# The last unit four heads at once, the last batch left by groups and transposes, the gate's choice moved, and buffers of their own for loaded weights

## Chip, cores, metric

The kernel runs on one core of one Trainium2 chip. The metric is the device time of one execution in microseconds; lower is better. All data are float32.

## What is computed

The input x is 8 batches of 1024 tokens of width 256. Cut to what matters:

```
x = x + 0.5 * ffn(layernorm(x))        # 8 experts, top-2 gate, capacity CAP
x = x + attn(layernorm(x))             # causal, 16 heads of 16
x = x + 0.5 * ffn(layernorm(x))

ffn:  probs = softmax(x @ gate_w.T); the two best experts of each token
      keep  = counts <= CAP            # CAP = 1.25 * 8192 / 8 = 1280
      an expert with counts > CAP gives nothing at all
attn: q,k,v = x@Wq.T+bq, x@Wkv.T+bkv;  softmax(q k^T / 4, causal) v;  @Wo.T + bo
```

Two choices per token make 16384 choices over 8 experts, 2048 on the mean, so with such data every expert is over its capacity and both ffn terms are zero. The kernel decides this on the chip: it counts the choices of both gates, and only where some expert is kept does it run the expert path, under `tc.If`. The profiled execution runs the attention and both counts, and no expert path.

## The kernel before

`attention` walks 32 **units**, four per batch b; unit u is group g = u mod 4, of four heads. A unit has 24 **steps**. `m_steps(u+1)` finds each query row's greatest score for the next unit: TensorE score tiles `sm`, then VectorE maxima (`first`, or a fused mask-add and maximum whose result lands in `top`). `settle` transposes the maxima (`pm`) and subtracts them from the queries (`qE`). `e_steps(u)` makes the scores again, transposed (`sc`), ScalarE takes the exponential into `pT`, GpSimd zeroes the part above the diagonal, and TensorE sums values and the softmax denominator into `pav`, for two halves `hf` of 512 query columns each.

A head is 16 wide plus one row for the maximum, so it takes 32 of TensorE's 128 rows. In a step, `scores(h)` is called for h = 0, 1 (two heads, pair `pr`), and between them `ms[k](h)` (two heads of the other pair). Both together use all four groups of 32 rows. In the last unit (u = 31) there is no next unit, so `ms[k]` is `None` and two heads alone are in a step. The values of a pair of steps are `owed` and done two and three steps later.

Other work goes **beside** the steps: generators that yield a number (wait so many steps), `PIECE` (a piece of TensorE work, begun when a step allows one) or `REST`. `Beside.step` runs what is due; `Beside.finish` runs a work to its end at once. The generators are `prepare`, `enter`, `values_of`, `residual` (load, normalise, project to values), `project` (queries and keys of two groups, spread to heads by DMAs from a tile `packed`), `gate_first` (first gate's choice), `leave` (divide by the softmax sums, project by Wo, add to x, store) and `regate` (second gate's choice). `choose` is the choice itself: maximum, softmax, then twice a best value, its lowest index and a one-hot row; some 20 VectorE instructions on 128x64 or 128x32 elements, parted by nine yields.

`leave(b, hf)` reads the 16 heads back from DRAM (`att_d`): sums, reciprocal, to DRAM (`inv_d`), back broadcast (`inv`), GpSimd multiply (`on`), then four `px` products over two chunks of 8 heads each. It is added at step 9 of g = 3 for the first half, and at step 2 of the next batch for the second. For the last batch, b = 7, the second half's `leave` and `regate` run after all units, by `drain`, followed by `any_kept` twice and the flag.

The opening sets up constants, `weights` loads and transposes Wk, Wq, Wv, Wo, and batch 0 is normalised and projected (two halves), before unit -1 with the `m_steps` of unit 0. Inside `attention` all of TensorE's, VectorE's, ScalarE's and GpSimd's instructions are kept in program order (`InOrder`); DMAs go in order on the queue of the engine that issues them. In the opening the query heads of the first group are spread by ScalarE's queue, all other heads by SyncE's:

```python
elif k < 4:
    (nc.sync if dsts is kTs else scalar).dma_start(out=to, in_=head)
else:
    others.append((to, head))
```

The loaded weights `wsb` share tag `packed`, four buffers of 128x512, with `project`. PSUM has six score banks and two of tag `bank` for all else.

Of the kernel before, what the change touches and what calls it, by code (L numbers as in the profile page):

```python
# [10 lines left out]
F32 = mybir.dt.float32  # L11
# [7 lines left out]
P = 128  # L19
# [81 lines left out]
def macaron_kernel(  # L101
# [59 lines left out]
    def mm(name):  # L161
# [16 lines left out]
    row16 = const.tile([P, 4], F32, name="row16")  # L178
    gpsimd.memset(row16, 0.0)
    gpsimd.affine_select(  # L180
        out=row16, in_=row16, pattern=[[-32, 4]], compare_op=ALU.not_equal, fill=1.0, base=-HD, channel_multiplier=1
    )
    one16 = const.tile([P, 1], F32, name="one16")
    vector.tensor_reduce(one16, row16, AX.X, ALU.max)
# [23 lines left out]
    def weights(pool, bank, matmul, transpose):  # L208
        def load(src, queue):
            wsb = pool.tile([P, DC, D], F32, tag="packed", name="wsb", bufs=4)  # L210
            queue.dma_start(out=wsb, in_=src.rearrange("(c p) d -> p c d", p=P))
            return wsb
# [15 lines left out]
        vector.tensor_scalar(bqT, bqT, QSCALE, None, ALU.mult)  # L228
# [98 lines left out]
    def choose(rp, tag, n, lg):  # L327
# [12 lines left out]
        yield 1  # L340
        sm = new("sm", (P, n))
# [7 lines left out]
        vector.scalar_tensor_tensor(key, key, 1e30, lc, ALU.mult, ALU.min)  # L349
        yield 1  # L350
        ohs = []
        for k in range(2):
            best = new("best", (P, n))
            vector.tensor_reduce(best, key, AX.X, ALU.max)
            cand = new("cand")
            vector.tensor_tensor(cand, key, over_e(best), ALU.is_equal)
            yield 1

            vector.scalar_tensor_tensor(
                cand, cand, -100.0, iota_e.unsqueeze(1).to_broadcast([P, n, E]), ALU.mult, ALU.add  # L360
            )
            first = new("first", (P, n))
            vector.tensor_reduce(first, cand, AX.X, ALU.min)
            yield 1
            oh = new(f"oh{k}")
            vector.tensor_tensor(oh, cand, over_e(first), ALU.is_equal)
            if k == 0:
                vector.scalar_tensor_tensor(key, oh, -1e32, key, ALU.mult, ALU.add)
            ohs.append(oh)
            yield 1  # L370
        both = new("both")
        vector.tensor_tensor(both, ohs[0], ohs[1], ALU.add)
        return prob, ohs, both
# [15 lines left out]
    def any_kept(layer, tally, ps):  # L389
# [5 lines left out]
        vector.tensor_scalar(counts, counts, float(CAP), None, ALU.is_le)  # L395
        some = route.tile([P, 1], F32, tag=f"some{layer}", name=f"some{layer}")
        vector.tensor_reduce(some, counts, AX.X, ALU.max)
        return some

    def flag(some, what):  # L400
        word = route.tile([P, 1], I32, tag="word", name=f"word_{what}")
        vector.tensor_copy(word, some)
        return nc.values_load(word[0:1, 0:1], min_val=0, max_val=1)


    def routing(layer, logits, wts, slots, idx):
        with tc.tile_pool(name=f"rt{layer}", bufs=1) as rp:
# [7 lines left out]
            prob, ohs, both = run(choose(rp, f"r{layer}", NT, logits))  # L415
# [247 lines left out]
    def attention(run_no, src, dst, gate0, logits, tally):  # L663
# [3 lines left out]
        with stack:  # L667
# [125 lines left out]
            def gate_first(b):  # L793
                if gate0 is not None:
                    lg = gate0[0][:, b * TB : (b + 1) * TB, :]
                    both = (yield from choose(ap_route, f"f{b}", TB, lg))[2]
                    vector.tensor_tensor(gate0[1], gate0[1], both, ALU.add)
# [3 lines left out]
            def project(u, apart, parts=(0, 512)):  # L801
# [3 lines left out]
                for s0 in parts:  # L805
                    others = []
                    for wT, bT, dsts, scale in ((wkT, bkT, kTs, 1.0), (wqT, bqT, qTs, QSCALE)):
# [14 lines left out]
                        for k in range(8):  # L822
# [3 lines left out]
                            if apart:  # L826
                                nc.sync.dma_start(out=to, in_=head)
                            elif k < 4:
                                (nc.sync if dsts is kTs else scalar).dma_start(out=to, in_=head)
# [51 lines left out]
            def e_steps(u):  # L881
# [28 lines left out]
                def values(hf, jb, pTs, part):  # L910
# [21 lines left out]
                    if jb == 4 * hf + 3 and part == 0:  # L932
# [70 lines left out]

            def regate(b, j0, j1):
# [10 lines left out]
                both = (yield from choose(ap_route, f"g{b}_{j0}", n, lg))[2]  # L1015
                vector.tensor_tensor(tally[:, j0:j1], tally[:, j0:j1], both, ALU.add)
# [60 lines left out]
            owed, light = deque(), deque()  # L1077
# [3 lines left out]
            for u in range(-1, NU):  # L1081
# [20 lines left out]
                if u > 0 and g == 0:  # L1102
                    beside.finish(valuing)
                    beside.add(gate_first(b))
# [10 lines left out]
                for k in range(STEPS) if u >= 0 else ():  # L1115
# [16 lines left out]
                    if g == 3 and u >= 0 and k == 9:  # L1132

                        beside.add(chain(leave(b, 0), regate(b, 0, HT) if b + 1 == B else ()))
# [14 lines left out]
                    beside.step(k in long_steps or u in (0, NU - 1) or beside.pending() > 1)  # L1149
# [5 lines left out]
            drain(leave(B - 1, 1))  # L1155
            drain(regate(B - 1, HT, TB))
            for e in (pe, vector, scalar, gpsimd):
                e.keep = False

# [3 lines left out]
    attention(0, x, out, (logits[0], tallies[0]), logits[1], tallies[1])  # L1163

    def kept_at_all(layer, tally):
        with ExitStack() as stack:
            ffn_banks(stack, f"count{layer}")
            return any_kept(layer, tally, acc(f"cnt{layer}"))

    somes = [kept_at_all(f"{k}", tallies[k]) for k in range(2)]  # L1170
    either = route.tile([P, 1], F32, name="either")
    vector.tensor_tensor(either, somes[0], somes[1], ALU.max)
    with tc.If(flag(either, "either") > 0):

        with tc.If(flag(somes[0], "0") > 0):
            feed_forward(0, logits[0], x, xw_d)
            tally = tally_tile("1b")
            attention(1, xw_d, out, None, logits[1], tally)
            vector.tensor_copy(somes[1], kept_at_all("1b", tally))
# [42 lines left out]
```

## Time and profile before

| | us |
|---|---|
| median of 3 runs | 1482.22 (1478.57 to 1483.34) |
| the profiled execution | 1481.55 |
| its span, first to last instruction | 1479.8 |
| TensorE busy | 1411.9 |
| VectorE busy | 1061.8 |
| ScalarE busy | 789.9 |
| GpSimd busy | 397.1 |

The table is of one execution. "Busy" is the sum of an engine's instructions; TensorE's ends are modelled, so its busy share does not say that it is at its peak. The chain of waits starts at the last instruction and goes back from each to what released it. In the groups and the timeline nearly every line of code reads L37, since a helper issues all instructions; the names of the tiles tell them apart. A number after x counts instructions, for TensorE in the chain weight loads and products together.

### The profile page before, as it was taken

The page shows a single profiled execution, that of the slowest core. Times are in us where ns is not written, and L with a number is a line of the kernel's source. Part 1 is how long each engine was busy: PE and PEld are TensorE (multiplying, and loading weights), DVE is VectorE, ACT ScalarE, POOL GpSimd, SP SyncE. Part 2 cuts the span into 40 slices and gives each one's busy share as a digit, 9 for nine tenths or more (in the row PEclk, how much of TensorE's full clock was granted, in tenths as well). Part 3 has the DMA queues.
Part 4 walks back from the last instruction along what each step waited for, and adds up shares of the span by engine and source line. Part 5 has one row for each costly group of instructions (what it writes and reads, how often), then busy time and mean ns, then how long its engine had stood idle before and what let it go on. Part 6 is the DMA issues. An engine that isn't in the chain of part 4 may idle for free.

```text
span 1479.8 us, 38173 instructions
## 1 busy us (share of the span) xinstructions
PE 1411.9 (95%) x14760; PEld 554.8 (37%) x14760; DVE 1061.8 (72%) x3395; ACT 789.9 (53%) x1790; POOL 397.1 (27%) x713
## 2 busy tenths in 40 slices
PE   5999999999999999999999999999999999999972
PEld 2434333343434333343333334343333434334320
DVE  2857678777877767777787777877677777778622
ACT  2255555555555565555555555555655556555640
POOL 2015114241143313142141411433131421321121
PEclk9999999999999999999999999999999999999995
DMA  4010111211021210212112111212112111121010
GB/s 138 9 37 23 37 33 43 67 58 47 29 62 55 69 37 32 64 41 80 31 46 66 58 45 30 64 49 72 37 32 62 42 51 31 47 66 37 23 61 32
DMA packets 58224, 71.93 MB, mean 49 GB/s; under 512 B 15912, under 2 KB 33456, under 8 KB 58032
## 3 DMA queue, kind: packets, MB, share of 16 engines
q1 hardware_dynamic: 56688, 68.60, 15.6%
q8 instruction: 118, 1.93, 0.5%
q10 hardware_dynamic: 1344, 0.79, 0.2%
q14 instruction: 74, 0.61, 0.1%
HBM read 26.88 MB, written 25.69 MB: 36 GB/s over the span
## 4 chain that ended last, share of the span: by engine, by line
PE 86%; DVE 6%; POOL 2%; ACT 2%; DMA 2%; issue 1%; SPq 0%; ACTq 0%; DVEq 0%; POOLq 0%
PE sc L37 39%; PE pav L37 20%; PE pq L37 8%; PE sm L37 7%; PE pv L37 4%; PE px L37 4%; DVE sm L37 2%; PE pm L37 2%; DVE qE L37 2%; PE pta L37 1%; ACT pT L37 1%; DMA att_d<-att 1%; POOL rstd_a L37 1%; POOL xa L37 1%; POOL pT L37 1%
## 5 line engine op out<-in xcount | busy, mean ns | idle before, releaser
L37 ACT ACTIVATE pT<-sc 128x512 f32<-128x512 f32 (+3 forms) x1536 | 669.3, 488 | 550.0 <-PE sm L37 448.0
L37 PE MATMUL sm<-kT,qT 32*128 32x512 f32 (+3 forms) x3072 | 786.1, 536 | 1.7 <-DVE top L37 0.5
L37 PE MATMUL sc<-qE,kT 32*128 32x512 f32 (+3 forms) x3072 | 736.6, 534 | 1.3 <-ACT pT L37 1.3
L37 POOL TENSOR_SCALAR_AFFINE_SELECT pT<-pT 128x256 f32<-128x256 f32 x512 | 207.1, 407 | 987.7 <-ACT pT L37 984.4
L37 DVE TENSOR_REDUCE first<-sm 128x1 f32<-128x512 f32 x512 | 328.7, 684 | 150.2 <-PE sm L37 147.2
L37 PE MATMUL pav<-pT,vaug 128*32 128x256 f32 (+2 forms) x5120 | 386.7, 371 | 1.7 <-POOL pT L37 1.7
L37 PEld LDWEIGHTS sc<-qE,kT 32*128 32x128 f32 x3072 | 261.4, 183 | 336.8 <-ACT pT L37 237.4
L37 DVE CUSTOM_DVE_ANT_0 sm<-sm,causal,first 128x256 f32<-128x256 f32 (+3 forms) x512 | 262.1, 555 | 94.2 <-PE sm L37 86.0
L37 PEld LDWEIGHTS sm<-kT,qT 32*128 32x128 f32 x3072 | 299.3, 184 | 23.6 <-DVE top L37 11.8
L37 DVE CUSTOM_DVE_ANT_0 sm<-sm,causal 128x256 f32<-128x256 f32 (+3 forms) x512 | 241.3, 514 | 72.0 <-PE sm L37 52.4
L37 PEld LDWEIGHTS pav<-pT,vaug 128*32 128x32 f32 x5120 | 102.7, 108 | 333.1 <-issue 221.6
L37 DVE DVE_READ_ACCUMULATOR2_ANT top<- 128x1 f32 x1024 | 144.5, 141 | 0.0
L37 PE MATMUL px<-woT,on 128*32 128x264 f32 x1024 | 81.8, 402 | 20.1 <-POOL on L37 18.2
L37 PE MATMUL pv<-wvT,xnT 128*32 128x264 f32 x1024 | 82.1, 393 | 1.7 <-DVE qE L37 1.6
L37 PE MATMUL pq<-xnT,wkT 128*32 128x512 f32 x512 | 69.7, 621 | 3.7 <-ACT xnT L37 3.7
L37 POOL TENSOR_SCALAR xn_a<-xa,mv_a,rstd_a 128x256 f32<-128x256 f32 x56 | 67.7, 1222 | 19.1 <-PE pta L37 19.0
L37 PE MATMUL pq<-xnT,wqT 128*32 128x512 f32 x512 | 66.8, 596 | 0.8 <-ACT packed L37 0.8
L37 PEld LDWEIGHTS px<-woT,on 128*32 128x32 f32 x1024 | 30.4, 112 | 55.2 <-POOL on L37 20.3
L37 DVE TENSOR_TENSOR qE<-qT,pm 128x512 f32<-128x512 f32 x64 | 43.5, 679 | 3.2 <-PE pm L37 2.3
L37 POOL TENSOR_TENSOR on<-on,inv 128x512 f32<-128x512 f32 x32 | 40.6, 1270 | 11.2 <-DMA inv<-inv_d 11.2
L37 PEld LDWEIGHTS pv<-wvT,xnT 128*32 128x32 f32 x1024 | 29.8, 110 | 36.6 <-issue 15.5
L37 POOL TENSOR_TENSOR xa<-xa,bo_all 128x528 f32<-128x528 f32 x32 | 41.8, 1307 | 2.8 <-issue 2.3
(113 smaller groups left out, 552.3 us busy)
## 6 DMA issues: line engine op xcount, KB each, us to landing
att_d<-att SPq DMA_DIRECT2D x64, 256.0 KB
kT<-packed SPq DMA_DIRECT2D x256, 32.0 KB
on<-att_d SPq DMA_DIRECT2D x32, 256.0 KB
inv<-inv_d SPq DMA_DIRECT2D x32, 256.0 KB
out_dram<-xa SPq DMA_DIRECT2D x16, 512.0 KB
qT<-packed SPq DMA_DIRECT2D x248, 32.0 KB
xa<-in_L_attn_x_dram SPq DMA_DIRECT2D x7, 1024.0 KB
xa<-in_L_attn_x_dram SPq DMA_DIRECT2D x2, 512.0 KB
```

The lines of the kernel that those rows point to most:

```text
L37: i = call(*args, **kwargs)
```

## The change

1. The last unit runs pairs of steps: the scores of both pairs `pr`, four heads, then the values owed from the pair of steps before.
2. The last batch leaves by groups of heads. `leave_first` divides and projects heads 0 to 7 in unit 30, both halves; `divided` treats heads 8 to 11 by the same way over DRAM; the last group, heads 12 to 15, does not go over DRAM: `leave_last` copies `pav`, transposes it, divides with the sum beside the values, transposes back and projects. The first half of it runs in unit 31, with its `regate` behind it.
3. `choose` finds the first one-hot row from `lc == 0` rather than from `key`, while the exponential runs; it has six yields instead of nine. `both` is gone, each one-hot row is added to the tally by itself. `gate_first(b)` of a later batch is added at step 9 of g = 0 rather than at its start.
4. In the opening: `one16` is made by GpSimd alone, the scaling of `bqT` goes from VectorE to GpSimd, the query heads are spread by SyncE's queue, and `wsb` has four buffers of its own.
5. The counts: `fewest` is taken inside `attention`, for the first gate ahead of the second half's `leave_last`, and the flag is written as an integer at once.

```diff
-    row16 = ...
-    vector.tensor_reduce(one16, row16, AX.X, ALU.max)
+    gpsimd.memset(one16, 0.0)
+    for k in range(4):
+        gpsimd.affine_select(out=one16, in_=one16, pattern=[[0, 1]], ..., base=-32 * k - HD, ...)
...
-            wsb = pool.tile([P, DC, D], F32, tag="packed", name="wsb", bufs=4)
+            wsb = pool.tile([P, DC, D], F32, tag="wsb", name="wsb", bufs=4)
...
-        vector.tensor_scalar(bqT, bqT, QSCALE, None, ALU.mult)
+        gpsimd.tensor_scalar(bqT, bqT, QSCALE, None, ALU.mult)
...
 choose:
+        def lowest(oh):
+            vector.tensor_tensor(cand, cand, iota_e..., ALU.add)
+            first = new("first", (P, n))
+            vector.tensor_reduce(first, cand, AX.X, ALU.min)
+            vector.tensor_tensor(oh, cand, over_e(first), ALU.is_equal)
+        vector.tensor_scalar(cand, lc, 0.0, -100.0, ALU.is_equal, ALU.mult)
+        lowest(ohs[0])
+        yield 1
         sm = new("sm", (P, n))
...
+        vector.scalar_tensor_tensor(key, ohs[0], -1e32, key, ALU.mult, ALU.add)
         yield 1
-        for k in range(2): ...
+        best = ...; cand = (key == best)
+        yield 1
+        vector.tensor_scalar(cand, cand, -100.0, None, ALU.mult)
+        lowest(ohs[1])
+        yield 1
+        return prob, ohs
...
 project:
-                            if apart:
+                            if apart or k < 4:
                                 nc.sync.dma_start(out=to, in_=head)
-                            elif k < 4:
-                                (nc.sync if dsts is kTs else scalar).dma_start(out=to, in_=head)
...
 values:
-                    if jb == 4 * hf + 3 and part == 0:
+                    if u == NU - 1 and jb == 4 * hf + 3:
+                        if part == 0:
+                            last.append(pav.pop(hf))
+                    elif jb == 4 * hf + 3 and part == 0:
...
+            def divided(b, hf, h0, h1, on, waits):
+                att_d, n = att_ds[b, hf], h1 - h0
+                sums = ...
+                yield waits[0]
+                nc.sync.dma_start(out=sums[: 8 * n], in_=att_d[h0:h1, HD, :]...)
+                nc.sync.dma_start(out=on[: HD * n], in_=att_d[h0:h1, :HD, :])
+                yield waits[1]
+                vector.reciprocal(sums[: 8 * n], sums[: 8 * n])
+                nc.sync.dma_start(out=inv_d[:n]..., in_=sums[: 8 * n])
+                yield waits[2]
+                nc.sync.dma_start(out=inv[: HD * n, 0, :], in_=inv_d[:n]...to_broadcast([n, HD, 512]))
+                yield waits[3]
+                gpsimd.tensor_tensor(on[: HD * n], on[: HD * n], inv[: HD * n, 0, :], ALU.mult)
+                yield 2
+
+            def leave_first(b, hf):
+                ...
+                yield from divided(b, hf, 0, 8, on[:, 0], (2, 3, 3, 3))
+                for i in range(HT):
+                    yield PIECE
+                    matmul_cols(px[:, : D + E], on[:, 0, i * P : (i + 1) * P], woT[:, 0, :])
+                    vector.tensor_tensor(xb[:, j, :], px[:, : D + E], xb[:, j, :], ALU.add)
+
+            def leave_last(b, hf, pav, copies):
+                gpsimd.memset(normed[:, :, : P // 2], 0.0)
+                for k in range(2):
+                    copies[k](att[:, k * 256 : k * 256 + 256], pav[:, k * 256 : k * 256 + 256])
+                yield PIECE
+                for i in range(4):
+                    transpose(pt[:, i * P : (i + 1) * P], att[:, i * P : (i + 1) * P])
+                vector.reciprocal(inv, heads[:, :, :, HD])
+                for i in range(4):
+                    vector.tensor_tensor(normed[:, i, P // 2 :]..., heads[:, i, :, :HD], inv..., ALU.mult)
+                yield PIECE
+                for i in range(4):
+                    transpose(pt[:, i * P : (i + 1) * P], normed[:, i])
+                for k in range(2):
+                    copies[k](on[P // 2 :, 1, cols], pt[P // 2 :, cols])
+                for i in range(4):
+                    yield PIECE
+                    matmul_cols(px[:, : D + E], on[:, 1, i * P : (i + 1) * P], woT[:, 1, :])
+                    vector.tensor_tensor(xb[:, j, :], px[:, : D + E], xb[:, j, :], ALU.add)
+                    ln_stats(xb, j, *gate_lns[b])
+                nc.sync.dma_start(out=dst[b, rows]..., in_=xb[:, hf * HT : hf * HT + HT, :D])
...
 the units:
+                for k in range(0, STEPS, 2) if u == NU - 1 else ():
+                    then = es[k + 1][1]
+                    for h in range(2):
+                        es[k][0](h)
+                        es[k + 1][0](h)
+                    owed.append((0, then, 0)); owed.append((0, then, 1))
+                    while len(owed) > 2:
+                        _, then, part = owed.popleft()
+                        then(part)
+                    if k == 0:
+                        beside.add(divided(b, 1, 8, 12, ons[1][:, 1], (1, 3, 3, 3)))
+                    if k == 2:
+                        beside.add(settle(u, 1), first=True)
+                    if k == 8:
+                        beside.finish(dividing)
+                        copies = (vector.tensor_copy, vector.tensor_copy)
+                        beside.add(chain(leave_last(b, 0, last.pop(), copies), regate(b, 0, HT)), first=True)
+                    for begin in (True, False):
+                        ...
+                        beside.step(begin)
-                for k in range(STEPS) if u >= 0 else ():
+                for k in range(STEPS) if 0 <= u < NU - 1 else ():
...
+                    if u == NU - 2 and k in (0, 3):
+                        beside.add(leave_first(b, k // 3))
+                    if u == NU - 2 and k == 9:
+                        dividing = beside.add(divided(b, 0, 8, 12, ons[0][:, 1], (2, 3, 3, 3)))
+                    if g == 0 and b and k == 9:
+                        beside.add(gate_first(b))
...
-            drain(leave(B - 1, 1))
+            leasts = [None if gate0 is None else fewest("0", gate0[1], bank("cnt0"))]
+            drain(leave_last(B - 1, 1, last.pop(), (scalar.copy, vector.tensor_copy)))
             drain(regate(B - 1, HT, TB))
+            leasts.append(fewest("1" if gate0 else "1b", tally, bank("cnt1")))
```

## Prediction

> **What bounds the kernel.** The page first: TensorE is nearly always busy, and its row of 40 slices is low only in the first and the last, where granted clock is low too.
>
> ```profile
> PE 1411.9 (95%) x14760; PEld 554.8 (37%) x14760; DVE 1061.8 (72%) x3395; ACT 789.9 (53%) x1790; POOL 397.1 (27%) x713
> ...
> PE   5999999999999999999999999999999999999972
> ```
>
> So units 0 to 30 are TensorE's, and the change works at both ends. Then the windows of unit 31 (first exponential to last `pav`), the tail, and the rest. Busy times of PE, PEld, DVE, ACT, POOL stand behind the length.
>
> ```profile
> 1401.61:1430.75 29.14, 28.49 (x262) 10.70 (x256) 1.51 (x4) 21.13 (x50) 6.98 (x17) 1.00 0.16 49
> 1430.75:1470.47 39.72, 11.42 (x130) 4.98 (x130) 17.65 (x74) 1.04 (x3) 7.04 (x8) 0.64 0.17 55
> 1470.47:1479.80 9.33, 0.00 (x0) 0.00 (x0) 0.01 (x1) 0.00 (x0) 0.00 (x0) 0.50 0.04 11
> ```
>
> In unit 31 TensorE is full, ScalarE 21.13 of 29.14. In the tail no engine is: a chain, 39.72 us long. The chain of waits (start, length) shows its middle: the second half's reciprocal runs only behind the first half's gate, then two trips over DRAM.
>
> ```profile
> 1414.71 1.06 PE sc L37 x4
> 1415.77 0.57 PE pav L37 x8
> ...
> 1445.13 0.47 DVE sums L37
> 1445.62 1.44 DMA inv_d<-sums
> ...
> 1447.71 4.90 DMA inv<-inv_d
> ...
> 1454.00 5.70 PE px L37 x56
> ```
>
> The same view of the opening: VectorE waits for 1 KB of `bqT` with batch 0's statistics queued behind it; `one` comes behind those, the `kT` copies behind `one`, the weights' copies behind the `kT` copies, and `pta` behind them at 16.13.
>
> ```profile
> 2.44 6.66 DMA bqT<-in_L_attn_bq_dram
> ...
> 13.53 0.05 DVE one L37
> ...
> 13.60 1.99 ACT kT L37 x2
> ...
> 16.13 1.98 PE pta L37 x8
> ```
>
> The timeline of ScalarE shows its queue issuing four DMAs with the next copy behind them:
>
> ```profile
> 24.71 2.53 ACTq L37 DMA_DIRECT2D qT<-packed  x4
> 27.27 1.07 ACT L37 COPY xnT<-pta 128x512 f32<-128x512 f32 x2 [2.64 <-DMA qT<-packed]
> ```
>
> **The Trainium skill.** "TensorEngine Tiling (Array Packing)", Key Properties: tiles operate independently, 32x128 giving four. The trace agrees: in unit 31 two 512-wide products (x4 with loads) take 1.06; in units before, four, two `sc` and two `sm`, take the same (0.62 and 0.41 at 1382.02). "TensorE: Matmul & The Clock Gate", Part 1: after some 3.4 us idle the clock halves. Agrees: `px` x56 takes 3.37 us at 1432.78, but 5.70 at 1454.00 behind 16.3 us of idling. "DMA: Bandwidth & Descriptors", Anatomy: about 2 us fixed. Agrees: `sums` issued at 1414.86 is used at 1416.96. "Perfetto Trace Analysis", Tensor Engine Instruction: ScalarE, VectorE and GpSimd are strict FIFO. The waits above show it.
>
> **Opening.** What goes: `bqT` and `one` leave VectorE, four DMA issues a half leave ScalarE. Without `bqT`, VectorE starts when x has landed. Traffic is about 350 GB/s from 3 us on; the first half of x and two weight tiles share it, so I estimate 5.7 us for the first half, 7.7 for the second. Eight statistics of 0.53 end at about 10.1. GpSimd now waits for `bqT` until 9.13 (its own queue ahead, memsets to 8.05 plus some 0.5 for `one16`, is done by then), and `ve_a`, `rstd_a` stand behind it: 9.13+0.25+0.25+1.04, with hand-offs 10.75. Two `xn_a` at 0.41 give `pta` at 11.6. `one16` needs five small GpSimd instructions (row select 0.19), so the `kT` and weight copies on ScalarE are done by 11.2 even if `one16` ends only with the memsets at 8 us (two `kT` copies 1.99, two weight copies 0.59 each). Pair by pair, two times 0.98 for `pta`, a copy, hand-offs: `pq` at 14.2 against 18.77: **-4.6**. Then 2.53 us of DMA issue leave ScalarE: -2.35 more. TensorE's gap before the second `pq` shrinks from 3.0 us to 0.7, so its clock may stay up: 32 products in 3.6 instead of 5.34. Now SyncE is the new limit: kT four issues 18.3 to 20.9, qT to 23.4 (0.63 each), landing 2 us later, 25.4; first `sm` before 33.67, now about 25.7. The second half's qT issues end at 33.5, landing 35.5; needed 10.8 us after the first `sm`, at 36.5: just covered. If that cover went, each microsecond that it is late goes onto the path, since TensorE's order is fixed. Own `wsb` buffers take away a wait that would now appear (`packed` of the second half behind the first half's DMAs); at the old pace none shows. The `sm` phase behind is VectorE's and only shifts. So the first `sm` moves by 8.0: **-8.0**, bounds -3.5 (x lands late, qT late) and -9.5.
>
> **Middle.** Instructions of a choice: 20 before, 20 after. Seven of eight gates of kind f move to steps 9 to 15. VectorE is 14.02 of 16 us busy at 588 to 604 (gate in it), 11.55 at 604 to 620. Unit starts, from the first exponentials: g = 0 units last 44.67, g = 2 units without a gate 44.43, and their first eight steps 12.8 and 13.2. So the gate costs nothing where it is; where it goes, a step lasts 2.1 to 2.5, two `first` take 1.37, the biggest burst is four times 0.22. **0**, bounds -3 and +5.
>
> **Unit 30** takes work out of the tail: 8 `px` of 4 products; 3.37 us per 28 products makes 0.48 each, **+3.9** on a full TensorE (bounds 3 and 6). Eight adds of 0.43 and four reciprocals fit, VectorE being 29.20 of 37.69 there. On SyncE `inv` waits for `inv_d`, on GpSimd `on` for `inv`, with `pT` selects behind it; three steps of 1.6 between each cover 2.4 and 4.0 us of transfer, nearly.
>
> **Unit 31.** Score time before: per step 1.06, 0.84, 0.63, 0.42 by width; 2x2.95 for half 0 and 2x(4x1.06+2.95) for half 1, 20.3. Four heads at once halve it, -10.1. Comes: eight transposes (0.66 per four) and four `px`, 3.2. TensorE 28.5-10.1+3.2=21.6. ScalarE: six exponentials in 3.11, so 0.52, 0.42, 0.33, 0.225 by width, four heads: 4x1.495+4x(4x0.52+1.495)=20.3. Neither can hide the other's hand-offs any more; I add 2.7 to TensorE's sum for them (the reciprocal's wait below, the first exponentials at the start and the last selects and values at the end): 24.3 for 29.14, **-4.8** (bounds -2.5 and -7.5). Waits added: VectorE's reciprocal of heads 8 to 11 waits for `sums` (exponentials 2.1, copy 0.6, two landings: about 7.4 into the unit), with half 0's `pav` copies behind it and, in TensorE's order, the transposes; ScalarE then has 2.1 us of exponentials to go on with. `on` for half 1 is needed only in the tail.
>
> **Tail**, from the last `pav`, T. Half 0's last `px` is begun at step 18, and behind it ScalarE still has the exponentials of steps 18, 20 and 22 (1.7, 1.3, 0.9), then a select (0.41) and values (0.36): so it lies at T-4.7, with a hand-off T-4.9. From there `px` 0.45, add 0.43, statistics 0.52, GpSimd's rstd 1.5 and 21 gate instructions of 0.222 carry VectorE to T+2.7; the first count's reductions 0.41 and half a copy 0.36 stand behind: T+3.5. ScalarE's half copy is done long before; the transposes of the other half wait. Four transposes, clock half down, 1.0; reciprocal and four products 1.1; transposes 0.4; copies 0.4; first `px` 0.9: T+7.3. Four times add and statistics 0.43+0.52: T+11.2. rstd 1.5; 21 gate instructions 4.7 (the exponential's 0.26 is hidden); count 0.75; reductions 0.43; flag 0.2: T+18.8. Before: 39.72. **-20.9**, bounds -16 (GpSimd or the clock slower than in these rows) and -24 (VectorE free when `pav` ends). The 9.33 behind stay: branch and its loads.
>
> **Sum**: -8.0+0+3.9-4.8-20.9=-29.8. Span 1479.8 to 1450.0; its execution 1481.55 to 1451.8; the runs' median lies 0.67 above that execution: **1452.4**.
>
> **Rivals.** (a) The opening stays: SyncE's queue or x's landing takes the place of the waits removed, 3.5 instead of 8.0: 1456.9. For it: eight more issues of 0.63 on one queue; against: the margins above. (b) Unit 31 and the tail meet each other: gate leftovers on VectorE hold the half copies, ScalarE bounds the unit: bounds -2.5, -16 and +6 there: 1461.7. (c) Slower: gates at steps 9 to 15 stall TensorE. The page's f groups sum to 41.8 us, 5.2 per batch; if VectorE had no room at all, 7x5.2=36.6 come on the path: 1489.0. It decides from 4.9 us a batch on ((29.8+4.4)/7, 4.4 being 0.3%). Against: 4.45 us of VectorE idle in that window, and six score banks that let TensorE run ahead. That the change does nothing needs the same at 4.2 us.
>
> **Chances.** Forecast 0.60, (a) 0.18, (b) 0.16, (c) 0.04, no change 0.02. 0.3%, 4.4 us, is about what a measurement here can tell from no change. The range from 1442 (opening -9.5, unit 31 -7.5, tail -24, middle -1.3) to 1464 takes in (a), (b) and a bit of the middle's cost. Faster 0.94, same 0.02, slower 0.04.
>
> **What would show it.** In the opening `pta` near 11.6 and the first `sm` near 25.7; no ACTq issue of qT. In unit 31 exponentials without gaps, unit of some 24 us. In the tail no `inv_d`, no idle over 4 us on TensorE before the transposes, and last count some 19 us behind the last `pav`. The middle's unit starts 44.67 apart as before. Wrong, if g = 0 units grow by over 1 us, if the first `sm` waits for a DMA, or if the tail exceeds 24 us.

## The result, and the profile after

The changed kernel takes 1459.39 us in the median (1457.61 to 1459.84); the kernel before, run beside it on the same chip, takes 1480.39 (1478.35 to 1483.34). The ratio is 0.9854 with an interval of 0.9832 to 0.9877: 1.5% faster. The prediction was 1452.4, from 1442 to 1464. The profiled execution after takes 1459.11 with a span of 1457.3; before it was 1481.55 and 1479.8.

The page of the kernel after, engines and the row of 40 slices. TensorE's busy time fell by 6.4 us only; of the slices the first and the last two changed (5, 7, 2 before).

```profile
PE 1405.5 (96%) x14776; PEld 552.5 (38%) x14776; DVE 1070.4 (73%) x3417; ACT 790.1 (54%) x1790; POOL 398.4 (27%) x719
...
PE   7999999999999999999999999999999999999994
```

The same three windows as before the change: unit 31, the tail, the rest. Behind the length stand the busy times of PE, PEld, DVE, ACT and POOL; the third column from the end is the granted clock.

```profile
1403.78:1433.08 29.30, 25.81 (x310) 11.19 (x304) 11.07 (x38) 20.16 (x50) 9.29 (x21) 1.00 0.11 38
1433.08:1450.34 17.26, 5.56 (x43) 2.41 (x42) 11.53 (x54) 0.97 (x3) 1.27 (x2) 0.71 0.09 30
1450.34:1457.30 6.96, 0.00 (x0) 0.00 (x0) 0.00 (x0) 0.00 (x0) 0.00 (x0) 0.50 0.05 14
```

Unit 31 is as long as it was (29.14), though TensorE is now busy for 25.81 us of it instead of 28.49, and VectorE for 11.07 instead of 1.51. The tail shrank from 39.72 to 17.26. Stage by stage, in microseconds of the two profiled executions:

| stage | before | after | difference | predicted |
|---|---|---|---|---|
| start to the first exponential of unit 0 | 62.24 | 56.36 | -5.9 | -8.0 |
| units 0 and 1 | 95.09 | 96.62 | +1.5 | 0 |
| units 2 to 29 | 1206.59 | 1211.08 | +4.5 | 0 |
| unit 30 | 37.69 | 39.71 | +2.0 | +3.9 |
| unit 31, to the last `pav` | 29.14 | 29.30 | +0.2 | -4.8 |
| tail, to the flag | 39.72 | 17.26 | -22.5 | -20.9 |
| rest | 9.33 | 6.96 | -2.4 | 0 |
| span | 1479.8 | 1457.3 | -22.5 | -29.8 |

The measured 1459.39 is 7.0 above the forecast, and it is inside the range because the tail carries it. Three stages gave less than promised: the opening by 2.1, the units between by 6.0, unit 31 by 5.0; unit 30, the tail and the rest gave 5.9 back. The chain of waits of the tail (start, length, engine, tile) shows what is left of it. It runs through engines only; no trip over DRAM is in it.

```profile
1434.85 0.16 DVE least L37
1435.01 0.33 DVE att_last L37
1435.41 0.44 PE pt_last L37 x2
...
1436.54 0.75 PE on_last L37 x4
...
1437.73 1.15 PE px_last L37 x8
```

VectorE's half of the copy `att_last` stands right behind the first half's gate and counts (`least`), in the place where the prediction had it; it starts 1.9 us after the last `pav` at 1433.08 (3.1 predicted), and the first `px_last` ends 5.8 us after it (7.3 predicted).

### The profile page after: what moved, and what is told of

It is laid out like the page before. It is cut to its first block, busy times and chain, and to the rows that moved or that the text cites. A ratio compares the mean times of both kernels' runs of the same rounds, so it can differ in the third digit from the quotient of the medians.

```text
span 1457.3 us, 38249 instructions
## 1 busy us (share of the span) xinstructions
PE 1405.5 (96%) x14776; PEld 552.5 (38%) x14776; DVE 1070.4 (73%) x3417; ACT 790.1 (54%) x1790; POOL 398.4 (27%) x719
## 4 chain that ended last, share of the span: by engine, by line
PE 85%; DVE 7%; POOL 3%; ACT 2%; DMA 2%; issue 1%; SPq 1%; ACTq 0%; DVEq 0%; POOLq 0%
PE sc L37 40%; PE pav L37 20%; PE pq L37 8%; PE sm L37 6%; PE pv L37 4%; PE px L37 4%; PE pm L37 2%; DVE sm L37 2%; DVE qE L37 2%; PE pta L37 1%; ACT pT L37 1%; DMA att_d<-att 1%; POOL rstd_a L37 1%; DVE first L37 1%; POOL xa L37 1%
## 5 line engine op out<-in xcount | busy, mean ns | idle before, releaser
L37 PE MATMUL px<-woT,on 128*32 128x264 f32 x960 | 76.1, 389 | 6.6 <-DVE qE L37 6.6
L37 POOL TENSOR_TENSOR on<-on,inv 128x512 f32<-128x512 f32 (+1 forms) x32 | 40.7, 1273 | 13.1 <-DMA inv<-inv_d 13.1
L37 PE MATMUL pm<-ident,top 128*128 128x128 f32 x256 | 42.5, 289 | 0.0
```

What stands on the lines that cost most here:

```text
L37: i = call(*args, **kwargs)
```

## The experiments

Each kernel below is the changed kernel with one edit, unless it says otherwise. A difference in a stage compares profiled executions, one each; medians are of all runs of a kernel. Where the code is the same, units 2 to 29 repeat within 0.3 us (eight kernels with the middle of the changed one take 1210.88 to 1211.18). Other stages repeat less well: the tail takes 17.26 to 17.85 in four kernels that share it, the first exponential comes between 55.3 and 57.0 in eight that share the opening, and unit 0 lasts from 54.4 to 58.5. The kernels were run in three groups, each beside the kernel before, which took 1481.44, 1480.43 and 1480.51 there (1480.39 above); so a difference of medians can be off by about 1 us for that reason alone. In the expectations, theory A is mine and B its rival. Three readings were to be tested: where the opening lost 2.1, what slowed units 2 to 29, and why unit 31 gained nothing.

**The opening: SyncE's queue.** The chain of waits of the opening, after:

```profile
10.49 0.42 DVE xn_a L37
...
11.05 1.96 PE pta L37 x8
...
13.67 5.31 PE pq L37 x32
...
31.70 1.87 DMA qT<-packed
...
33.71 4.00 PE sm L37 x8
```

`pta` starts at 11.05 instead of 16.13 and `pq` at 13.67, both a little better than predicted; the first `sm` came at 24.70. Then the chain passes into SyncE's queue: the second half's query heads are issued from 31.70 on, and the eight `sm` products that need them take 4.00 us, while the heads are issued 0.6 us apart. Ahead of these issues the queue holds eight heads of the second group (`others`), which nothing needs yet. This kernel issues them behind the second half's first group:

```diff
-                    for to, head in others:
-                        nc.sync.dma_start(out=to, in_=head)
+                    later.extend(others)
+                    while s0 and later:
+                        to, head = later.pop(0)
+                        nc.sync.dma_start(out=to, in_=head)
```

> The changed kernel, but in the opening the heads of the second group (others) of both halves are issued on SyncE's queue only behind the first group's heads of the second half. Theory A (SyncE's queue holds the second half's queries: in the changed kernel sm waits some 3 us for qT, issued at 31.70 to 34.13): those issues come 5 us earlier, the gap in TensorE between 31 and 36 us goes, the clock stays up, unit 0's first exponential moves from 56.36 to about 53, the whole by -3 us. Rival B (the sm phase is bound by VectorE's maxima and only waits somewhere else): the first exponential stays within 0.7 us of 56.36 and the whole within 1 us.

Measured: 1454.78 (1454.5 to 1458.73), 4.6 less than the changed kernel. The first exponential comes 2.3 earlier, in a profiled execution that was the slowest of this kernel's four. Its timeline:

```profile
28.03 2.43 SPq L842 DMA_DIRECT2D qT<-packed  x4
...
34.14 2.09 PE L37 MATMUL sm<-kT,qT 32*128 32x512 f32 x8
```

The issues are 3.7 us earlier, and the same eight products take 2.09. In the three kernels with these late `others` the first exponential comes at 53.3 to 54.9, in the eight without at 55.3 to 57.0. So the queue was the wait, and its 2.3 us are what the opening lost. TensorE's granted clock falls with it, to 0.50 from 35 to 40 us in all eight, against 0.59 to 0.83 in the three; how much of the 2.3 is the wait itself and how much the clock, these runs do not part.

The opening's edits together, undone (VectorE's `bqT` and `one16`, tag `packed` for `wsb`, ScalarE's queue for the first query heads):

```diff
-        gpsimd.tensor_scalar(bqT, bqT, QSCALE, None, ALU.mult)
+        vector.tensor_scalar(bqT, bqT, QSCALE, None, ALU.mult)
-                            if apart or k < 4:
+                            if apart:
                                 nc.sync.dma_start(out=to, in_=head)
+                            elif k < 4:
+                                (nc.sync if dsts is kTs else scalar).dma_start(out=to, in_=head)
...
```

> The changed kernel with the opening as before: row16 and VectorE's reduction for one16, bqT scaled by VectorE, query heads of the first group on ScalarE's queue, wsb in the buffers of packed. Theory A (the opening's edits bring 6 us to the first exponential, and unit 0 gives 1 to 2 back at a lower clock): pta at 16.1, first sm at 33.7, first exponential at 62.2, unit 0 at 55.8; the whole +4 to +6. Rival B (the gain is lost later, something else sets unit 0's pace): the whole within 1 us.

Measured: 1468.27 (1462.9 to 1470.9), +8.9. `pta` is back at 16.16, the first `sm` at 33.89, the first exponential at 63.56 (+7.2). By stage the four edits are worth the gain that the table shows, and somewhat more; the median says more than the 4 to 6 that were expected, with runs 8 us apart. Apart from the queue below, the four were not taken one by one.

Only ScalarE's queue for the first query heads restored:

```diff
-                            if apart or k < 4:
+                            if apart:
                                 nc.sync.dma_start(out=to, in_=head)
+                            elif k < 4:
+                                (nc.sync if dsts is kTs else scalar).dma_start(out=to, in_=head)
```

> The changed kernel, but in the opening the first group's query heads are issued on ScalarE's queue as before. Theory A (the move trades a wait of ScalarE for one of SyncE's queue): the first sm comes 2.5 us later, at 27.2, but the second half's queries are there in time, no gap between 31 and 36, first exponential within 1 us of 56.4, the whole within 1 us. Rival B (the move is a clear gain): first exponential at 58.5 to 59, the whole +2 to +3. Rival C (the move is a loss, SyncE's backlog weighs more): first exponential at 54 to 55, the whole -1.5 to -2.5.

Measured: 1462.13 (1457.29 to 1462.79, 5 runs), +2.7 in the median. But the profiled run was its quickest by 4.4 us, the other four lying from 1461.7 to 1462.8, and in that one the first exponential comes at 53.97, 2.4 earlier than with SyncE. The windows from 30 to 40 us, first of the changed kernel, then of this one:

```profile
30.00:40.00 10.00, 9.57 (x46) 4.13 (x44) 6.49 (x26) 0.37 (x1) 0.00 (x0) 0.53 0.22 53
```

```profile
30.00:40.00 10.00, 9.69 (x68) 4.29 (x67) 9.57 (x36) 2.92 (x5) 0.00 (x0) 1.00 0.15 37
```

The granted clock is 0.53 in one and 1.00 in the other, though TensorE is busy 96% and 97%. The low clock there is not chance, since all eight kernels with the changed opening have it (at 0.50 from 35 to 40 us); but of this kernel only the quickest of five runs was profiled, and its other four do not look like it. None of the three theories fits both the stage and the median, and which queue is the better one is not settled by these runs.

**The units between: bursts of VectorE.** Unit starts lie 44.56 apart for g = 0 (44.67 before), 43.06 for g = 1 (43.06), 45.16 for g = 2 (44.43), 40.70 for g = 3 (40.71). Most of the loss is in g = 2, 0.5 to 0.7 in each of six units; unit 29 is 1.06 longer and unit 1 0.87. In g = 2 `regate` of the previous batch runs, in the steps with the widest maxima, and it uses the same `choose`. VectorE's timeline in step 3 of such a unit (unit 14), start and length first:

```profile
678.06 0.41 DVE L37 TENSOR_SCALAR cand_g<-cand_g 128x64 f32<-128x64 f32 x1
678.50 0.23 DVE L37 TENSOR_TENSOR cand_g<-cand_g,iota_e 128x64 f32<-128x64 f32 x1
678.76 0.22 DVE L37 TENSOR_REDUCE first_g<-cand_g 128x8 f32<-128x64 f32 x1
679.02 0.23 DVE L37 TENSOR_TENSOR oh_g<-cand_g,first_g 128x64 f32<-128x64 f32 x1
679.22 0.69 DVE L37 TENSOR_TENSOR qE<-qT,pm 128x512 f32<-128x512 f32 x1
```

Four instructions of the choice between two yields take 1.2 us, and behind them on VectorE stands `settle`'s `qE`. TensorE's only idle time in this unit is a wait for that `qE`. The first line is from the changed kernel, the second is the same place in unit 14 of the kernel before:

```profile
679.97 0.65 PE L37 MATMUL pv<-wvT,xnT 128*32 128x264 f32 x8 [0.75 <-DVE qE L37]
```

```profile
682.70 0.65 PE L37 MATMUL pv<-wvT,xnT 128*32 128x264 f32 x8 [0.27 <-DVE qE L37]
```

The window of that step in the changed kernel:

```profile
678.52:681.34 2.82, 2.07 (x30) 0.78 (x32) 2.70 (x11) 0.87 (x2) 0.41 (x1) 1.00 0.19 47
```

VectorE is busy 2.70 of 2.82, TensorE 2.07: in this step VectorE is the bound. The step lasts 2.33 before, so it holds 0.49 of the 0.73 by which 45.16 exceeds 44.43; the rest is in step 0 (2.35 against 2.11), where three instructions for `key` stand together. Two kernels part the reasons. The first takes the choice as it was before, with its nine yields, but `gate_first` at the new place; the second keeps the new choice and its order, and has nine yields instead of six, three of them new and two moved, so that no more than three instructions stand between two:

```diff
 lowest:   cand = cand + iota; first = min(cand)
+          yield 1
           oh = (cand == first)
...
+        yield 1
         vector.scalar_tensor_tensor(key, ohs[0], -1e32, key, ALU.mult, ALU.add)
-        yield 1
         best = new("best", (P, n))
         vector.tensor_reduce(best, key, AX.X, ALU.max)
+        yield 1
         vector.tensor_tensor(cand, key, over_e(best), ALU.is_equal)
+        vector.tensor_scalar(cand, cand, -100.0, None, ALU.mult)
         yield 1
-        vector.tensor_scalar(cand, cand, -100.0, None, ALU.mult)
-        lowest(ohs[1])
+        yield from lowest(ohs[1])
```

> The changed kernel with choose as it was: the old order of operations and nine yields, both one-hot rows still added to the tally one by one, gate_first still at step 9. Theory A (choose's steps of three and four VectorE instructions, where regate meets the 512-wide maxima at the start of g = 2, hold TensorE): units with g = 2 fall from 45.16 back to 44.43, over six of them -4.4 us; the tail gets some 0.5 us longer for the two exponentials; the whole -3.5 to -4.5. Rival B (the moved gate_first shifts pieces of later units, so g = 2 suffers for it): g = 2 stays at 45.1 and the whole within 1 us, or +0.5.

> The changed kernel with choose in its new order of operations, but with more yields: at most two VectorE instructions in a step where the changed kernel has four, and the key's last step apart. Theory A (it is the number of small VectorE instructions in one step that holds TensorE, not their order): g = 2 units at 44.4, unit 1 at 39.3, units 2 to 29 at 1204 to 1205 instead of 1211.1, the tail as in the changed kernel, 17.8; the whole -6 to -7. Rival B (the order does it, with one operation more before the second choice): g = 2 units stay at 45.1, the whole within 1 us.

Measured: the old choice 1453.23 (1452.73 to 1455.44), -6.2; the new one with more yields 1452.16 (1450.81 to 1452.46), -7.2. Units 2 to 29 take 1204.40 and 1204.17 instead of 1211.08, unit 1 39.27 and 39.24 instead of 40.14, and units of g = 2 are back at 44.43 and 44.41. A whole unit 14 of the second kernel holds the same work as in the changed kernel, where it lasts 45.16 with 44.41 of TensorE:

```profile
668.16:712.57 44.41, 44.15 (x492) 16.23 (x493) 31.20 (x101) 25.70 (x58) 6.52 (x16) 1.00 0.19 55
```

So it is neither the order of the instructions nor their number, but where the yields part them: how many stand together ahead of `qE`. In both kernels TensorE's wait for it in unit 14 is back at 0.27 and 0.26. Units of g = 0, where `gate_first` now stands ahead of a `qE`, gain too, from 44.56 to 44.32 and 44.31 (the wait in unit 4 falls from 0.63 to 0.38 and 0.37); the forecast of the first kernel had left these and unit 1 out. A `qE` issued ahead of the choice was not tried. In the tail, where nothing is beside it, the old choice takes 1.4 us more (18.68), the new one with nine yields no more than the spread (17.58): there the new form is the shorter chain.

The old choice with `gate_first` back at the start of g = 0 as well:

```diff
                 if u > 0 and g == 0:
                     beside.finish(valuing)
+                    beside.add(gate_first(b))
...
-                    if g == 0 and b and k == 9:
-                        beside.add(gate_first(b))
```

> The run with choose as before, and gate_first back at the start of g = 0 too. Theory A (moving the gate to step 9 by itself spares a third of a microsecond a batch): g = 0 units from 44.32 back to 44.67, units 2 to 29 from 1204.4 to 1206.6. Rival B (where the gate stands makes no difference): 1204.4 stays. Rival C (at step 9 it does harm): below 1204.

Measured: 1454.87 (1452.24 to 1457.33); units 2 to 29 take 1206.49 against 1204.40, and units of g = 0 44.66 against 44.32. Moving `gate_first` gains about 0.3 a batch, 2.1 in all. The medians, 1.6 apart with ranges that overlap, agree with that and would not show it alone.

**Unit 31: queues, not work.** The timeline of the changed kernel, at the end of the unit:

```profile
1428.77 1.04 POOL L37 TENSOR_TENSOR rstd_g<-ve_g,half 128x4 f32<-128x4 f32 x1
1429.78 0.77 POOL L37 TENSOR_SCALAR_AFFINE_SELECT pT<-pT 128x256 f32<-128x256 f32 x2
...
1430.24 0.99 PE L37 MATMUL pav<-pT,vaug 128*32 128x256 f32 x8 [1.16 <-POOL pT L37]
...
1430.71 0.23 ACT L37 ACTIVATE prob_g<-lc_g 128x32 f32<-128x32 f32 x1 [1.61 <-DVE lc_g L37]
1430.85 0.76 ACT L37 ACTIVATE pT<-sc 128x128 f32<-128x128 f32 x4
```

The first half's gate stands in two queues ahead of the attention. GpSimd's `rstd_g` comes before the selects, and TensorE's values wait 1.16 us for those. ScalarE waits 1.61 us for the gate's `lc_g`, with the last exponentials behind it. Both engines take their instructions in order, which is what the Trainium skill says of them ("Perfetto Trace Analysis", Tensor Engine Instruction). Four kernels take the unit apart.

First, all of the old leaving with the new unit, four heads at once:

```diff
-                        beside.add(chain(leave_last(b, 0, last.pop(), copies), regate(b, 0, HT)), first=True)
+                        beside.add(chain(leave(b, 0), regate(b, 0, HT)))
...
-            drain(leave_last(B - 1, 1, last.pop(), (scalar.copy, vector.tensor_copy)))
+            drain(leave(B - 1, 1))
```

(also without `leave_first` and `divided` in units 30 and 31)

> The changed kernel, unit 31 still by pairs, but the last batch leaves as before: all 16 heads over DRAM, the first half from unit 31's step 8 on, the second behind the last unit, each with its regate. Theory A (the two trips over DRAM, the reciprocal behind the first half's gate and a cold TensorE make the tail): tail back from 17.8 to about 40, unit 30 back to 37.7, unit 31 some 2 to 3 shorter; the whole +17 to +19. Rival B (the tail is mostly the gate's own chain, the way of leaving matters little): +5 at most.

Measured: 1473.49 (1469.38 to 1476.79, 11 runs), +14.1. The windows of its unit 31 and tail:

```profile
1404.24:1429.52 25.28, 24.39 (x260) 10.32 (x253) 1.24 (x2) 20.32 (x50) 6.73 (x17) 1.00 0.17 56
1429.52:1467.70 38.18, 11.17 (x133) 5.09 (x132) 16.25 (x73) 1.04 (x3) 7.06 (x8) 0.72 0.18 57
```

Four heads at once alone bring unit 31 from 29.14 to 25.28, -3.9. The new leaving and the first half's gate put 4.0 back into it (29.30), and take 20.9 out of the tail. Its tail is 1.5 shorter than before too: in its chain each of the two gates takes 4.4 instead of 4.9, and the last `px` 5.12 instead of 5.70. The median is 14.1 higher where 17 to 19 was expected; unit 31 gave 4.0 where 2 to 3 was expected.

Second, both halves' `regate` in the tail:

```diff
-                        beside.add(chain(leave_last(b, 0, last.pop(), copies), regate(b, 0, HT)), first=True)
+                        beside.add(leave_last(b, 0, last.pop(), copies), first=True)
...
-            drain(regate(B - 1, HT, TB))
+            drain(regate(B - 1, 0, TB))
```

> The changed kernel, but the last batch has one regate over all eight token tiles at the very end, none for its first half in unit 31. Theory A (the tail hangs on VectorE's gate instructions of the first half: att_last's second copy at 1434.93 is behind them, and the last exponentials wait for the gate's exponential): 21 instructions of 0.2 leave the chain, the last values end 1 to 1.5 us earlier, the final gate's instructions are on 128x64 and 0.03 longer each; flag at about 1447.5 instead of 1450.2, the whole -2.5 to -3. Rival B (last values end on their own time and the copies wait for them): -1 at most. Rival C (the longer final gate costs more than is saved): +0.5.

Third, the same with the values lagging two pairs of steps behind the scores instead of one, and `leave_last` added two steps later for that reason:

```diff
-                    while len(owed) > 2:
+                    while len(owed) > (4 if k else 2):
...
-                    if k == 8:
+                    if k == 10:
                         beside.add(leave_last(b, 0, last.pop(), copies), first=True)
```

> The run with one regate for the last batch at the end, and in unit 31 values two pairs of steps behind their scores instead of one. Theory A (in unit 31's first half the values wait for exponential and select of the pair just before, and TensorE's fixed order hands that wait to the next scores): unit 31 from 27.7 to about 25.5. Rival B (ScalarE bounds the unit, and the values left for its end are more): 27.5 to 28.5.

Measured: 1458.69 (1456.88 to 1459.31) and 1455.32 (1454.94 to 1456.08). Unit 31 lasts 27.66 and 25.88, and the tail (17.26) hardly changes, by -0.6 and -0.4 us: one gate over eight chunks there costs no more than one over four behind the leftovers of the other. By stage the first gains 2.3, near the 2.5 to 3 expected; its median shows 0.7, and its profiled execution has a unit 0 that is 1.9 longer. With the gate gone from the unit, the values that waited 1.16 us for the selects wait 0.33, and the last eight exponentials follow each other without a gap. The window of unit 31 in the third kernel:

```profile
1404.19:1430.07 25.88, 24.78 (x309) 11.19 (x303) 8.22 (x24) 19.83 (x49) 8.03 (x19) 1.00 0.11 35
```

By its records TensorE is busy 24.78 of 25.88 again, with the transposes and `px` in it; ScalarE, which the prediction had at 20.3, is busy 19.83.

Fourth, unit 31 with one pair of heads a step and values two and three steps later, as before, under the new leaving:

```diff
-                for k in range(0, STEPS, 2) if u == NU - 1 else ():
+                for k in range(STEPS) if u == NU - 1 else ():
...
-                        es[k][0](h)
-                        es[k + 1][0](h)
+                        scores(h)
-                    while len(owed) > 2:
+                        owed.append((now + 2, then, 0))
+                        owed.append((now + 3, then, 1))
+                    while owed and owed[0][0] <= now:
```

> The changed kernel, but unit 31 runs its steps one by one as before, two heads at a time, values two and three steps later; the last batch's leaving and the first half's regate stay beside it. Theory A (four heads at once halve 20 us of TensorE's score time, but unit 31 took up 3.2 us of leaving, hand-offs between ScalarE, GpSimd and TensorE in the first half and the gate's exponential, so it shows 29.3 instead of 24.3): single steps cost 3 to 5 us more. Rival B (the unit is bound by ScalarE's exponentials and hand-offs whichever way the scores come, four heads at once bring nothing): within 1 us. Rival C (pairs are worse, the one pair of lag makes values wait for selects): -1 to -3.

Measured: 1461.17 (1459.38 to 1465.11). Unit 31 lasts 32.40 (+3.1) and the tail 1.4 more, +4.5 by stage; the median shows +1.8, and in the profiled execution unit 0 was 2.1 shorter. Four heads at once are worth their 3 to 4 us under either leaving.

**All together.** The edits of the late `others`, the nine yields, one `regate` in the tail and the lag of two pairs, in one kernel; and the same with `regate` of the other batches moved to step 9 of g = 2:

```diff
-                        beside.add(chain(leave(b - 1, 1), regate(b - 1, 0, TB)))
+                        leaving = beside.add(leave(b - 1, 1))
...
+                    if g == 2 and b and k == 9:
+                        beside.finish(leaving)
+                        beside.add(regate(b - 1, 0, TB))
```

> The changed kernel with four edits together: others issued late in the opening, choose in the new order with more yields, one regate for the last batch, values two pairs behind in unit 31. If the parts add up as each showed by its stage (first exponential -1 to -2.3, units 1 to 29 -7.8, unit 31 -3.4, tail -0.4): flag at about 1437.5, median 1447. If the parts share a cause (TensorE's clock in the opening, hand-offs at the end): 1449 to 1451.

> The run with four edits, and regate of a batch b - 1 added at step 9 of g = 2 of batch b instead of behind its leave. Theory A (a gate costs least in steps 9 to 15, as gate_first showed, 0.35 us a batch): g = 2 units from 44.4 to about 44.1, and g = 1 a little shorter, whole -2. Rival B (values and projections of the next batch stand there in g = 2, VectorE has no more room than at the start): g = 2 longer, +1 to +3.

Measured: 1443.58 (1443.47 to 1446.57), ratio to the kernel before 0.9762 (0.9736 to 0.9788); and 1444.54 (1444.31 to 1446.67). From 1459.39 the medians' -4.6, -7.2 and -4.1 make 1443.5. That they meet so closely is luck: the five runs lie at 1443.5 and 1446.4, and by stages 1447 was expected. By stages units 1 to 31 did as expected, and the opening and unit 0 gave 5.1 where 2.3 at most was counted. The later `regate` takes 2.9 out of units 2 to 29, puts 1.05 into unit 30, and the rest went in a slower opening; it makes no difference that these runs can tell. Units of g = 2 became longer, 44.91 instead of 44.41, as rival B had it (TensorE waits 0.48 for `qE` there instead of 0.27), those of g = 1 shorter, 42.30 instead of 43.06. The first of the two, 1.1% below the changed kernel, is the version to keep.

## Why the prediction was right or wrong

- **Opening, -8.0; -5.9.** VectorE and ScalarE were freed as worked out. The step that failed is "needed 10.8 us after the first `sm`, at 36.5: just covered". I had taken the time from a maximum of those products (44.5) where the product itself starts at 42.41, 8.7 behind the first `sm` at 33.67. With 8.7 behind the measured first `sm`, 24.70, the need is at 33.4, and issues that end near 34 and land 2 us later are late. The queue that I named as the new limit was the limit, and lateness did go onto the path: 2.3 us by stage, 4.6 by the medians.
- **Middle, 0; +6.0 with units 0 and 1.** The step that failed is the inventory: "seven of eight gates of kind f move" looked at `gate_first` only. `choose` also serves `regate`, which did not move and stands beside the widest maxima. I had even called the units of g = 2 "without a gate", while VectorE's timeline of the kernel before has `best_g` in unit 14 at 677.37; so that "the gate costs nothing where it is" did not follow from the two kinds of unit, and at the start of g = 0 it cost 0.34 more than at step 9. I counted instructions (20 and 20), and saw the burst of "four times 0.22" only for the gate that moves, where it mattered how many stand ahead of `qE`. Without unit 0, whose length follows TensorE's clock, the loss is 5.4, just outside the bound of +5. The gate that moved gained 2.1.
- **Unit 30, +3.9; +2.0.** The term was mis-sized: it charged the eight `px` in full on a full TensorE, and the unit grew by half of that. The last of the eight begins at 1403.9, in unit 31; the others cost 2.0, or 2.3 against the 37.45 of the kernel with the old leaving, so 0.3 each. Where the rest hides was not tried. The count behind the 0.48 is misread twice: `px` x56 in the chain is 56 products, not products and loads together (the timeline has 56 of each), and a `px` over one chunk is eight products, not four. The two nearly cancel: groups of four start 0.22 apart in unit 30, 0.45 for a `px`.
- **Unit 31, -4.8; +0.2.** The gain of four heads at once was right in kind (-3.9 alone). The failed term is "I add 2.7 for hand-offs". With the old leaving, where by the same reckoning ScalarE's 20.3 is the larger sum (it measures 20.32), the unit lasts 25.28: the hand-offs are already 5.0. In the changed kernel two waits were not in the term: the first half's gate, whose `rstd_g` and exponential stand at the head of GpSimd's and ScalarE's queues (1.65 of unit 31 go with it), and values that follow their selects one pair of steps behind (1.8). Taking both away gives 25.88, still 1.6 above the predicted 24.3. TensorE's records sum to 25.81 where 21.6 was reckoned; they can hold waits, so how much of that is work stays open.
- **Tail, -20.9; -22.5.** The chain was the one predicted, gate leftovers of half 0 included. Of the 1.6 on top, 1.2 lies ahead of the copies: half 0's last `px` ends 5.9 us before the last `pav`, not 4.5, so the leftovers were done sooner after it. Since unit 31 ended 5.0 later than predicted, part of this gain is likely unit 31's loss under another name; that is argued. From the copy to the first `px` it took 3.95 against 4.2.
- **Rest, 0; -2.4.** Booked as unchanged. The flag is now written as an integer at once, but that is not the reason: with the same flag this stage takes 9.63 in the kernel with the opening undone, 9.16 in the one with ScalarE's queue and 8.77 in the one with the later `regate`. In the kernel before and in the first two of these SyncE pauses 2.1 to 2.5 us between two semaphore instructions behind the branch, in the changed kernel it does not. What makes it pause is open, so these 2.4 us cannot be credited to the change.
- **The sum.** The stages miss by +2.1, +6.0, -1.9, +5.0, -1.6 and -2.4. The three that help are a term sized too high, in part a shift from the stage before, and a stage that the change is not shown to move: luck in so far; the range did not need them, since without the last 2.4 the time would still be inside. The lower end of the range is a wrong sum: the four bounds named for it make 1443.8, not 1442.
- **Rivals.** The measured time lies between rival (a), 1456.9, and rival (b), 1461.7. Gates at steps 9 to 15 do not make g = 0 longer (44.56 against 44.67): rival (c) is false. The meeting in unit 31 was real, its place being the queues of GpSimd and ScalarE rather than VectorE alone. The rival of SyncE's queue was real in kind: it cost 2.3 of the 4.5 that it was given.

## What to carry to other kernels

Before an edit to a shared helper is booked at nothing, list all who call it and the step in which each runs; a burst of four small instructions stalls a full engine where its operand stands behind the burst, and the same work in shorter pieces does not. When work is moved beside a full engine, look on every in-order queue for what it puts ahead of the critical instructions, since a short instruction that waits for its input holds all behind it. When DMAs are gathered on one queue, order them by when they are needed, and take that time from the instruction that reads the data, not from a later one.

## What the runs showed of the hardware

TensorE's clock makes unit 0 vary from execution to execution. In eight profiled kernels that share the opening it lasts from 54.4 to 58.5 us. Two of them differ only in unit 31 and the tail; their windows from 55 to 60 us, first of the kernel with one `regate` (unit 0: 58.38), then of the one with single steps (54.42):

```profile
55.00:60.00 5.00, 5.00 (x24) 1.82 (x23) 2.50 (x12) 1.19 (x2) 0.42 (x1) 0.50 0.00 0
```

```profile
55.00:60.00 5.00, 5.00 (x41) 2.09 (x39) 4.06 (x16) 3.07 (x7) 0.82 (x2) 1.00 0.00 0
```

The granted clock is 0.50 and 1.00, and TensorE's busy time, 5.00 of 5.00 in both, does not tell the two apart. The Trainium skill ("TensorE: Matmul & The Clock Gate", Part 1) says that the window in which activity is judged runs freely, so that the slow phase of the same kernel differs between runs. The runs here agree that it differs; that the window is the reason, and why the clock is halved on a TensorE that its records show as busy, they do not show.

So an edit in the opening that is worth under 4 us is to be judged by the medians of several runs and by the stage that it changes, not by the span of one execution: the kernel with late `others` gained 2.3 in the first exponential and 4.6 in the median, but 0.3 in the span of its profiled execution.
